# Later keys and counts, and thirteen transfers issued by other engines, in a sparse attention layer on one core

## The chip, the core and the metric

The kernel runs on one core of one Trainium2 chip. TensorE (PE) multiplies matrices, VectorE (DVE), ScalarE (ACT) and GpSimd (POOL) work on tiles in SBUF, and SyncE (SP) issues transfers. ScalarE and GpSimd can issue transfers too; the rows ACTq, POOLq and SPq of a profile are the instruction queues of these engines. Each engine takes its instructions in order and waits for others by semaphores, so a waiting instruction holds up all that stands behind it on its engine. The metric is the device time of one execution in microseconds (us), lower is better.

## The reference

The layer normalizes x (2708 rows of 1024, float32), clips it at zero, and lets each row attend to its neighbours in a sparse 0/1 matrix `adj` of 2708 x 2708, whose entries are one with probability 0.0014771, so about four to a row:

```python
h = jnp.maximum(_layernorm(x, axis=-1), 0.0)
q = h @ W_q.T + b_q;  k = h @ W_k.T + b_k;  v = h @ W_v.T + b_v
z = scale * (q @ k.T) * adj
z = jnp.where(z == 0.0, -10000.0, z)
out = x + relu(softmax(z, axis=1) @ v)
```

(The last lines are shortened to the same computation.)

## The kernel before, in words

Rows come in 22 tiles of 128 (the last has 20). The kernel never forms k or v. It first multiplies the two weights into one 1024 x 1024 matrix M (rows of `wq` and `wk` are loaded in eight pieces each, `wq_sb[o]` and `wk_sb[o]`), so that a row's q is h M plus a row made from the biases. The two bias columns `bk_sb` and `bq_sb` are loaded by GpSimd at the start; VectorE scales them (L508, L509) and sums the pieces of `wk` with them into `acc_b`. Beside that it runs small set-up operations (L155 to L182).

At the same time the neighbours are found. Tiles of `adj` are loaded in the order SEARCH. For the tile at place k of it, `counted(k)` lets ScalarE sum the ones, `found(k)` lets VectorE find up to eight ones in each quarter of a row (L376), and `listed(k)`, at the end of a batch of up to four tiles, merges them into a row's sorted list of keys (L389 to L395). `counts` then counts each row's neighbours and prepares a table row: up to 16 neighbours, the row's number, the count (L645 to L653). `sort` finds each row's position by its count, with two small matmuls on TensorE (L662, L664); `put` (L613) scatters the table rows to `tab_dram` in this order, and `reload` (L625) brings the sorted table back, for the early eight tiles and the other fourteen apart. From there, a tile holds rows with about as many neighbours.

The products are done for pairs of tiles, in ten units n of kind q (q = h M) and ten of kind o (the output weight), one tile alone at the end. `multiply` does each pair in a seven-product scheme on 2 x 2 blocks: `blocks` forms sums of the input blocks (`s1` to `s4`, L688) from transposed tiles, of which ScalarE copies some (`a11`, `a12`, `a22`, L684) and one stays in PSUM; the products' results are joined on VectorE (for q at L1029 and L1032). Units 0 to 3 take tiles 0 to 7 in their natural order, later ones gather sorted rows of h.

Attention runs as a stream beside the products (`attention`, moved on by `advance`): for a sorted tile it gathers each row's neighbours into slots g (L597), takes their products with q (`scores`, L826), an exponential on ScalarE, and the weighted sum u (`weights`, `sums`, L871 and L879). A finished u is kept in SBUF if its output unit is near, else it is stored to `u_dram` by GpSimd (L888) and loaded again by SyncE (`or`, L1142). Ten are stored. Gathers from `h_dram` and the scatter of the results to `out` are GpSimd's.

What stands where is partly written out by hand: `steps_at[n, i]` is a string of steps that `follow` carries out after the i-th point of unit n. A letter is a step and the number its place: `f` found and listed, `i` found alone, `j` listed alone, `p` counted, `c` counts, `o` sort, `w` put, `z` and `b` reload, `g` a sum of squares. The order on VectorE is the order of the program there; that of SyncE and of PE comes from a scheduler that goes by its own estimates, and GpSimd's is partly held.

Of the kernel before, what the change touches and what calls it, by code (L numbers as in the profile page):

```python
# [18 lines left out]
P = 128  # L19
# [10 lines left out]
EARLY = 8  # L30
# [33 lines left out]
def tile_preln_masked_attention(  # L64
# [366 lines left out]
            ts_done[:] = [nc.vector.tensor_sub(t[k], a, b)]  # L431

    with tc.tile_pool(name="w", bufs=1, side="left") as wp:
        nc.gpsimd.dma_start(bk_sb, bk)
        nc.gpsimd.dma_start(bq_sb, bq)
        wq_sb = [wlow[:, o] for o in range(H)] + [wp.tile([P, D], FT, name=f"wq{o}") for o in range(H, DC)]
        wk_sb = [wlow[:, H + o] for o in range(H)] + [wp.tile([P, D], FT, name=f"wk{o}") for o in range(H, DC)]
        for o in range(DC):
            nc.sync.dma_start(wq_sb[o], wq_rows[o * P:(o + 1) * P, :])
            part = slice(0, NB) if o == 0 else slice(0, D)  # L440
            (nc.scalar if o < 2 else nc.sync).dma_start(wk_sb[o][:, part], wk_rows[o * P:(o + 1) * P, part])
            if o == 1:
                nc.scalar.dma_start(wk_sb[0][:, NB:], wk_rows[:P, NB:])

        t1 = [work.tile([P, D], FT, tag="hT", name=f"t1_{k}", bufs=2) for k in range(2)]

# [174 lines left out]
    def reload(lo, hi):  # L621

        full = min(hi, FULL)
        src = tab_dram[lo >= EARLY]
        loads = [nc.gpsimd.dma_start(ptab[:, lo:full, :], src[:(full - lo) * P, :].rearrange("(t p) w -> p t w", p=P))]  # L625
        if hi > FULL:
            loads.append(nc.gpsimd.dma_start(ptab[:REST, FULL, :], src[(FULL - lo) * P:, :]))
        for load in loads:
            for put in puts[lo >= EARLY]:
                tc.add_manual_dep(load.ins, put.ins.name,  # L630
                                  mybir.DependencyInfo(mybir.DependencyClass.Sync, mybir.DependencyReason.DATA),
                                  reason="every row of the part")
        return loads[-1]
# [82 lines left out]
    def natural_rows(n):  # L716
# [23 lines left out]
    steps_ahead = {(1, 5): "o1", (3, 6): "o0"}  # L740

    slots, free = [], []
# [1 line left out]
    def searched():  # L744
        search.close()

        att = ph.enter_context(tc.tile_pool(name="att", bufs=1, side="right", reuse_waits="tile"))
        for i in range(HIGH):
            slots.append(att.tile([P, D], FT, name=f"g{i}"))


        for c in range(4):
            for k, (i, j) in enumerate(((0, 0), (0, 1), (1, 1), (1, 0))):
                nc.sync.dma_start(slots[2 * c + k // 2][:, k % 2 * NB:(k % 2 + 1) * NB], wv[j][:, i * 4 + c, :])
        assert len(adj_loads) == NT
        free.extend([M.rearrange("p i j (a c) w -> p i j a (c w)", a=2)[:, 0, 1, a, :] for a in range(2)] + slots[8:])
# [118 lines left out]
    def sums(t):  # L875
        u, coef = us.pop(t)
        for s in range(0 if t in EMPTY else 1, K[t]):
            fill()
            chained(lambda: nc.vector.scalar_tensor_tensor(  # L879
                u, g_of[t][s], coef[:, at[t][s]:at[t][s] + 1], u, op0=ALU.mult, op1=ALU.add))  # L880
            free.append(g_of[t][s])
            yield 1.3
        fill()
        g_of.pop(t)
        if near(t):
            held[t] = u
        else:
            nc.gpsimd.dma_start(u_dram[t * P:(t + 1) * P, :], u)  # L888
        done.add(t)

    def marked(lo, hi):
# [268 lines left out]
    for n, unit in enumerate(units):  # L1160
        kind, ta, tb = unit
        now[0] = n
        if n == FIRST:
            ordered.close()
            ordered.enter_context(tc.manual_schedule(engines={mybir.EngineType.DVE}))
            nc.sync.dma_start(bp_dram, bp_sb[0:1, :])
        turn = n in (0, FIRST - 1)
        share = (20.0 if kind == "q" else 19.0) / 7
        nxt = units[n + 1] if n + 1 < len(units) else None
        results = (q_results if kind == "q" else o_results)(ta, tb)  # L1170

        def after(i):
            if (n, i) in steps_ahead:
                follow(steps_ahead[n, i])
            if (n, i) == (2, 5):
                owe(8)
                owe(9)
                rows_of[FIRST] = load_rows(units[FIRST])
                owe(10)
                owe(6)  # L1180
                owe(7)
                rows_of[FIRST + 1] = load_rows(units[FIRST + 1])
                pooled.close()
            if (n, i) in ((FIRST, 1), (FIRST, 5)):
                ts_of_wv(i // 2, i // 2 + 2)
            if (n, i) == (FIRST, 5):
                next(stream)
            if (n, i) == (FIRST, 6):
                chain.append(behind[-1])
                next(stream)  # L1190
                nc.vector.tensor_tensor(bad, bad, total, op=ALU.not_equal)
            if (n, i) == (FIRST + 1, 6):
                marked(EARLY, NT)
            if (n, i) == (FIRST + 2, 4):
                nc.vector.tensor_scalar(msq, msq, MLIMIT, None, op0=ALU.is_gt)
            if n > FIRST + 1 or n == FIRST + 1 and i > 1:
                advance(share)
            if nxt is not None:

                if i == (3 if n == 0 else 4 if turn else 0):  # L1200
                    ops_of[n + 1] = blocks(*rows_of[n + 1], nc.gpsimd if n + 1 < FIRST - 1 else None)
                    with tc.issue_after(products[-1].ins) if n + 1 == FIRST else nullcontext():
                        ops_of[n + 1][1]()
                if i == (4 if n == 0 else 5 if turn else 2):
                    ops_of[n + 1][2]()
                    rows_of.pop(n + 1)
                    if n == last_q - 1:
                        all_rows()
                if i == 3:
                    banks_of[n + 1] = banks_for(bp_sb)  # L1210
                if i == 6 and n + 2 < FIRST:
                    natural_rows(n + 2)
                if i == (2 if n in (FIRST, last_q) else 4) and n + 2 > FIRST and n + 2 < len(units) and n + 2 not in rows_of:
                    while units[n + 2][0] == "o" and not done.issuperset(units[n + 2][1:]):
                        advance(1.0)
                    rows_of[n + 2] = load_rows(units[n + 2])
            if (n, i) in steps_at:
                follow(steps_at[n, i])
            if (n, i) == (3, 4):
                searched()  # L1220
                for s in range(8, HIGH):
                    for c in range(0, D, D // 4):
                        clear = nc.gpsimd.memset(slots[s][:, c:c + D // 4], 0.0)
                        tc.add_manual_dep(clear.ins, counted_at[-1].ins.name,
                                          mybir.DependencyInfo(mybir.DependencyClass.Sync, mybir.DependencyReason.DATA),
                                          reason="not beside the counts")
            if i == 3 and units[n - 1][0] == "o" and NT - 2 in units[n - 1][1:]:
                tail(NT - 1)
            if nxt is None and i == 1:
                while alone not in done:  # L1230
                    advance(1.0)
                r, = load_rows(("o", alone))
                single["turned"] = turned(r, "alone")
            if nxt is None and i == 3:
                single["banks"] = banks_for(bp_sb)
            if n == last_q - 1 and i == 4:

                nc.sync.dma_start(bp_sb, bv.to_broadcast([P, D]))
                nc.vector.tensor_sub(bp_sb[:, NB:], bp_sb[:, NB:], bp_sb[:, :NB])

            for k, at in enumerate(((0, 0), (0, 1), (0, 3), (0, 4), (0, 5), (0, 6), (1, 2))):
                if (n - last_q, i) == at:
                    place, src = ((M[:, 0, 0], of_wv(0, 0)), (T[:, 0], tv_dram[0]), (T[:, 1], tv_dram[1]),
                                  (M[:, 1, 0], of_wv(1, 0)), (M[:, 1, 1], of_wv(1, 1)), (T[:, 2], tv_dram[2]),
                                  (T[:, 3], tv_dram[3]))[k]
                    nc.sync.dma_start(place, src)

        multiply(n, results, after)
# [231 lines left out]
```

## Time and profile before

| | |
|---|---|
| time, median of three runs | 648.64 us (646.54 to 648.71) |
| profiled execution, its time | 648.43 us |
| its span | 646.7 us |
| TensorE busy | 636.7 us, 98% |
| VectorE busy | 523.1 us, 81% |
| GpSimd busy | 400.1 us, 62% |
| ScalarE busy | 280.0 us, 43% |
| transfers | 189.02 MB, mean 292 GB/s |
| granted clock of TensorE, mean | 0.996 |
| chain of waits, share of the span | PE 75%, DVE 15%, DMA 6% |

The span runs from the first to the last instruction of the profiled execution; the time also holds what lies around it. A row of the timeline gives start, length, engine, line and operation, what it writes and reads, and in brackets how long its engine was idle ahead of it and what ended that. DMA issues are listed with the number of transfers, the size of each and the time from issue to landing. The engine of a matmul's weights is PEld.

### The profile page before, as it was taken

The numbers are of one execution on the slowest core, as the hardware profiler recorded it, in microseconds if no ns is written. First come the engines' busy times: TensorE is split into PE (matmuls) and PEld (weight loads), VectorE is DVE, ScalarE is ACT, GpSimd is POOL, SyncE is SP. The second block draws the span as 40 slices with busy tenths as digits, with TensorE's granted clock in tenths as the row PEclk, the third lists the DMA queues.
The fourth block names the chain that finished last, engine by engine and source line by source line (L and its number), as shares of the span: only waits on it lengthen the run. The fifth ranks groups of instructions, "written<-read, shape, count | busy, mean of one in ns | idle before, by whom it ended". The sixth has DMA issues, their size and how long they took to land.

```text
span 646.7 us, 6378 instructions
## 1 busy us (share of the span) xinstructions
PE 636.7 (98%) x1730; PEld 326.6 (51%) x1730; DVE 523.1 (81%) x1014; ACT 280.0 (43%) x426; POOL 400.1 (62%) x428
## 2 busy tenths in 40 slices
PE   9999999999999899999999999999999999999995
PEld 5777776454444445444444454444544544444442
DVE  5999599997896664999888969987999999988121
ACT  3448876858766532323223133332432434323200
POOL 2649990885767457865845536655785858782431
PEclk9999999999999999999999999999999999999998
DMA  8994999599799969998877999988898989884641
GB/s 337 407 355 143 391 342 393 202 322 353 244 343 311 360 196 402 352 374 263 302 277 267 419 414 315 289 264 261 242 332 274 289 297 322 256 281 122 168 140 69
DMA packets 61012, 189.02 MB, mean 292 GB/s; under 512 B 9711, under 2 KB 10047, under 8 KB 60074
## 3 DMA queue, kind: packets, MB, share of 16 engines
q0 software_dynamic: 31728, 98.74, 46.4%
q1 hardware_dynamic: 27514, 84.04, 35.1%
q10 hardware_dynamic: 1728, 5.77, 2.3%
q8 instruction: 16, 0.26, 0.2%
q14 instruction: 26, 0.21, 0.1%
HBM read 159.81 MB, written 42.31 MB: 313 GB/s over the span
## 4 chain that ended last, share of the span: by engine, by line
PE 75%; DVE 15%; DMA 6%; issue 2%; POOL 1%; ACT 0%; POOLq 0%; SPq 0%; DVEq 0%
PE ps L948 41%; PE psy L948 29%; DMA adj<-in_adj_dram 5%; PE pt L402 5%; DVE at L376 5%; DVE acc_b L519 2%; DVE st L224 1%; DMA bq_sb<-in_bq_dram 1%; DVE wlow L530 1%; DVE wlow L431 1%; DVE M L481 1%; DVE wlow L528 1%; DVE cand L394 1%; DMA h_dram<-x 0%; DVE s L688 0%
## 5 line engine op out<-in xcount | busy, mean ns | idle before, releaser
L597 POOL DMA_INDIRECT g<-h_dram,tab x105 | 127.0, 1209 | 60.7 <-issue 21.6
L948 PE MATMUL ps<-M,a 128*128 128x512 f32 x320 | 144.0, 593 | 0.1
L948 PE MATMUL psy<-wlow,s 128*128 128x512 f32 x320 | 143.9, 593 | 0.0
L826 DVE SCALAR_TENSOR_TENSOR junk<-g,pq 128x1024 uint8<-128x1024 f32 x93 | 113.7, 1223 | 7.6 <-DMA g<-h_dram,tab 5.7
L879 DVE SCALAR_TENSOR_TENSOR u<-g,coef,u 128x1024 f32<-128x1024 f32 x79 | 101.3, 1283 | 5.6 <-ACT u L871 3.6
L948 PEld LDWEIGHTS ps<-M,a 128*128 128x128 f32 x320 | 59.4, 190 | 68.2 <-issue 67.6
L948 PEld LDWEIGHTS psy<-wlow,s 128*128 128x128 f32 x320 | 59.3, 190 | 67.2 <-issue 66.8
L376 DVE FIND_INDEX8 at<-ones,adj 128x8 uint32<-128x685 f32 (+1 forms) x88 | 74.5, 865 | 0.0
L948 PE MATMUL ps<-wlow,s 128*128 128x512 f32 x160 | 72.0, 593 | 1.7 <-DVE s L688 1.7
L948 PE MATMUL psy<-wlow,a 128*128 128x512 f32 x160 | 72.2, 593 | 0.0
L948 PE MATMUL ps<-M,s 128*128 128x512 f32 x160 | 71.9, 592 | 0.0
L355 ACT ACTIVATE sized<-adj 128x2708 uint8<-128x2708 f32 (+1 forms) x22 | 54.3, 2467 | 13.7 <-DMA adj<-in_adj_dram 12.8
L1047 POOL DMA_INDIRECT y<-in_x_dram,tab x19 | 35.0, 1840 | 28.7 <-ACT y L1064 12.1
L285 POOL TENSOR_TENSOR hsum<-hsum,x 128x256 f32<-128x256 f32 (+1 forms) x56 | 38.6, 727 | 21.6 <-DVE wlow L431 15.6
L948 PEld LDWEIGHTS ps<-wlow,s 128*128 128x128 f32 x160 | 30.3, 190 | 40.3 <-issue 37.3
L948 PEld LDWEIGHTS psy<-wlow,a 128*128 128x128 f32 x160 | 30.4, 190 | 37.8 <-issue 37.3
L948 PEld LDWEIGHTS ps<-M,s 128*128 128x128 f32 x160 | 30.4, 190 | 37.8 <-issue 37.3
L778 POOL DMA_INDIRECT out_dram<-y,tab x21 | 29.8, 1419 | 18.1 <-DMA y<-in_x_dram,tab 10.5
L597 POOL DMA_INDIRECT M<-h_dram,tab x20 | 25.6, 1281 | 13.3 <-ACT u L871 4.6
L684 ACT COPY a<-pt 128x512 f32<-128x512 f32 x60 | 33.3, 589 | 1.1 <-PE pt L402 1.1
L613 POOL DMA_INDIRECT tab_dram<-tab,pos_i x22 | 22.4, 1017 | 17.5 <-DVE pos_i L673 12.0
L688 DVE TENSOR_TENSOR s<-a,pt 128x512 f32<-128x512 f32 x40 | 25.6, 680 | 6.7 <-ACT a L684 6.7
(240 smaller groups left out, 863.8 us busy)
## 6 DMA issues: line engine op xcount, KB each, us to landing
adj<-in_adj_dram SPq DMA_DIRECT2D x21, 1354.0 KB, 10.8
x<-in_x_dram SPq DMA_DIRECT2D x21, 512.0 KB, 7.4
h_dram<-x POOLq DMA_DIRECT2D x16, 512.0 KB, 7.4
q_late<-q SPq DMA_DIRECT2D x12, 512.0 KB, 6.4
pq<-q_late SPq DMA_DIRECT2D x12, 512.0 KB, 6.3
u_dram<-u POOLq DMA_DIRECT2D x10, 512.0 KB, 7.2
or<-u_dram SPq DMA_DIRECT2D x10, 512.0 KB, 7.6
g<-in_wv_dram SPq DMA_DIRECT2D x16, 256.0 KB, 9.6
```

Source lines behind the costliest of these rows:

```text
L285: small.append(nc.gpsimd.tensor_add(hsum[:n, cols], hsum[:n, cols], xt[:n, cols]))
L355: nc.scalar.activation(sized[:n], a[:n, :, :PW], AF.Abs, accum_out=total[:n, t:t + 1])
L376: nc.vector.max_index(at[:n, k - first_k, g, :], ones[:n, 0:8], a[:n, g, :])
L402: nc.tensor.transpose(pt[:, c, :], xt[:, k * P:(k + 1) * P], ident)
L597: return nc.gpsimd.indirect_dma_start(out=dst, out_offset=None, in_=src, in_offset=off, bounds_check=N - 1, oob_is_err=False)
L684: nc.scalar.copy(ops[name], bank)
L688: step = (eng or nc.vector).tensor_tensor(ops[name], a, b, op=op)
L778: to = nc.gpsimd.indirect_dma_start(out=out, out_offset=bass.IndirectOffsetOnAxis(ap=ptab.bitcast(U32)[:n, t, SLOTS:SLOTS + 1], axis=0), i ...
L826: chained(lambda: nc.vector.scalar_tensor_tensor(junk, g_of[t][s], 1.0, tq[t], op0=ALU.mult, op1=ALU.mult, accum_out=zall[:, t, s:s + 1]))
L879: chained(lambda: nc.vector.scalar_tensor_tensor(u, g_of[t][s], coef[:, at[t][s]:at[t][s] + 1], u, op0=ALU.mult, op1=ALU.add))
L948: mm = nc.tensor.matmul(bank, a[:, c, :], b[:, c, :], start=False, stop=(c == 3), skip_group_check=True)
L1047: return nc.gpsimd.indirect_dma_start(out=y[:n], out_offset=None, in_=x, in_offset=off, compute_op=ALU.add)
```

## The change

Four things are changed:

- The listing of the last batch of keys and the counts of the early half move in unit 3. The search of the last `adj` tile stays at (3, 1), its listing goes to (3, 5), and the counts go there from (3, 2). The zeroing of three gather slots, which waits for the counts, goes from (3, 4) to (3, 5).
- The two biases are loaded by ScalarE, behind its three loads of `wk`, instead of by GpSimd.
- The early table is loaded by SyncE instead of by GpSimd; the other table stays with GpSimd.
- The stores of u are issued by SyncE instead of by GpSimd.

```diff
     with tc.tile_pool(name="w", bufs=1, side="left") as wp:
-        nc.gpsimd.dma_start(bk_sb, bk)
-        nc.gpsimd.dma_start(bq_sb, bq)
...
             if o == 1:
                 nc.scalar.dma_start(wk_sb[0][:, NB:], wk_rows[:P, NB:])
+                nc.scalar.dma_start(bk_sb, bk)
+                nc.scalar.dma_start(bq_sb, bq)
...
-        loads = [nc.gpsimd.dma_start(ptab[:, lo:full, :], src[:(full - lo) * P, :].rearrange("(t p) w -> p t w", p=P))]
+        loads = [(nc.gpsimd if lo >= EARLY else nc.sync).dma_start(ptab[:, lo:full, :], src[:(full - lo) * P, :].rearrange("(t p) w -> p t w", p=P))]
...
-                (3, 1): "f21", (3, 2): "c0", (3, 3): "p21", (3, 5): "g0", (3, 6): "w0-7 g1 g2 g3 g4", (4, 4): "b0"}
+                (3, 1): "i21", (3, 3): "p21", (3, 5): "j21 c0 g0", (3, 6): "w0-7 g1 g2 g3 g4", (4, 4): "b0"}
...
         else:
-            nc.gpsimd.dma_start(u_dram[t * P:(t + 1) * P, :], u)
+            nc.sync.dma_start(u_dram[t * P:(t + 1) * P, :], u)
...
             if (n, i) == (3, 4):
                 searched()
+            if (n, i) == (3, 5):
                 for s in range(8, HIGH):
                     for c in range(0, D, D // 4):
                         clear = nc.gpsimd.memset(slots[s][:, c:c + D // 4], 0.0)
```

On VectorE, in unit 3, behind the search of the last `adj` tile, two pieces of the difference (the number behind a tile's name is a buffer's; `cand` are the candidates of a row, `q` the results of tiles 6 and 7, `s` the sums for the next pair):

```order
 L376 MAX_INDEX at<-ones,adj_155 128x8 x4
+L1032 TENSOR_TENSOR q_1351<-ps_1257,u_1362 128x512
+L1029 TENSOR_TENSOR q_1352<-psy,p_1335 128x512
+L688 TENSOR_TENSOR s_1442<-a_1435,pt 128x512
+L688 TENSOR_TENSOR s_1444<-a_1385,pt 128x512
+L688 TENSOR_TENSOR s_1446<-s_1442,a_1385 128x512
+L688 TENSOR_TENSOR s_1448<-a_1392,s_1446 128x512
 L389 TENSOR_TENSOR cand<-first,at 128x128
 L390 SCALAR_TENSOR_TENSOR cand<-at,cand 128x128
```

The two results and the four sums now stand right behind the search. Where they stood, behind the last operation of the counts and ahead of the sort, is this piece:

```order
 L650 TENSOR_TENSOR sort<-deg,down 128x144
 L653 TENSOR_SCALAR tab<-keys 128x8x16
-L1032 TENSOR_TENSOR q_1351<-ps_1257,u_1377 128x512
-L1029 TENSOR_TENSOR q_1352<-psy,p_1335 128x512
-L688 TENSOR_TENSOR s_1477<-a_1470,pt 128x512
-L688 TENSOR_TENSOR s_1479<-a_1408,pt 128x512
-L688 TENSOR_TENSOR s_1481<-s_1477,a_1408 128x512
-L688 TENSOR_TENSOR s_1483<-a_1415,s_1481 128x512
 L666 COPY sort<-ps_all 128x144
```

The twenty-one rows of keys and counts, from L389 to L653, have changed places with six rows of results and sums.

On VectorE at the start, the set-up operations among the sums with the biases (`t` are differences of halves of `wk`):

```order
 L525 TENSOR_TENSOR t_0_199<-wlow 128x512
 L519 SCALAR_TENSOR_TENSOR acc_b<-wlow,bq_sb,acc_b 128x1024
+L155 CAST tab<-zall 128x22
+L158 CAST past<-zall 128x22
+L165 CAST down<-zall 128x20
+L181 CAST first<-zall 128x32
+L159 TENSOR_SCALAR past<-past 128x22
 L525 TENSOR_TENSOR t_0_199<-wlow 128x512
+L182 MEMSET zall 128x352
```

These six stood ahead of the first operation that reads a bias, and now stand behind the second sum with them.

On SyncE, near the end, where three of the ten stores of u now stand (u_3325, u_3438 and u_3493 are those of tiles 20, 18 and 19; `or` are loads of stored u, of the same tiles in the same order; `pq` are loads of q for the scores):

```order
 L799 DMA pq_3351<-q_late 128x1024
 L799 DMA pq_3406<-q_late 128x1024
+L888 DMA u_dram<-u_3325 128x1024
 L799 DMA pq_3445<-q_late 128x1024
+L888 DMA u_dram<-u_3438 128x1024
 L1142 DMA or_3557<-u_dram 128x1024
+L888 DMA u_dram<-u_3493 128x1024
 L1142 DMA or_3700<-u_dram 128x1024
 L1142 DMA or_3702<-u_dram 128x1024
```

The store of tile 18 now stands ahead of the load of tile 20, and that of tile 19 ahead of the load of tile 18.

## The prediction

> **What bounds the kernel now.** I read the page first, then the busy time by stretch, then what TensorE waited for, then the rows around that wait. The page says how full each engine is:
>
> ```profile
> span 646.7 us, 6378 instructions
> PE 636.7 (98%) x1730; PEld 326.6 (51%) x1730; DVE 523.1 (81%) x1014; ACT 280.0 (43%) x426; POOL 400.1 (62%) x428
> ```
>
> A busy PE is not yet a PE at its pace, so I take the stretches (us, then busy time of PE, PEld, DVE, ACT, POOL, then the granted clock, DMA share, GB/s) and the waits of PE (total, times, longest):
>
> ```profile
> 106.00:212.00 106.00, 104.27 (x296) 49.58 (x295) 92.31 (x256) 75.00 (x94) 75.37 (x119) 1.00 0.86 305
> 212.00:630.00 418.00, 418.00 (x1162) 198.98 (x1163) 338.67 (x549) 137.88 (x247) 253.28 (x205) 1.00 0.85 288
> ...
> PE ps L948 <- DVE s L688: 1.7, 1, 1.7
> PE ps_y L498 <- POOL hsum L112: 1.2, 1, 1.2
> ```
>
> From 212 to 630 us TensorE is busy for 418.00 of 418.00 us at a clock of 1.00: there, nothing that VectorE, GpSimd or a transfer does earlier can shorten the kernel. Before that PE waits twice: 1.2 us at the very start, for a memset, and 1.7 us once, for VectorE's s. The change can win at this second wait, and else it can only lose. These are the rows of that place on PE and on VectorE (start, length, what; the idle time ahead in brackets):
>
> ```profile
> 206.59 3.60 PE L948 MATMUL ps<-M,a 128*128 128x512 f32 x8
> 211.86 3.70 PE L948 MATMUL ps<-wlow,s 128*128 128x512 f32 x8 [1.67 <-DVE s L688]
> 215.40 3.60 PE L948 MATMUL psy<-wlow,a 128*128 128x512 f32 x8
> 218.84 0.23 PE L662 MATMUL ps_in<-sort,before 128*128 128x144 bf16 x1
> ...
> 205.29 0.29 DVE L389 TENSOR_TENSOR cand<-first,at 128x128 f32<-128x128 f32 x1
> ...
> 209.80 0.22 DVE L653 TENSOR_SCALAR tab<-keys 128x128 uint32<-128x128 f32 x1
> 209.94 0.68 DVE L1032 TENSOR_TENSOR q<-ps,u 128x512 f32<-128x512 f32 x1
> 210.54 0.68 DVE L1029 TENSOR_TENSOR q<-psy,p 128x512 f32<-128x512 f32 x1
> 211.13 1.27 DVE L688 TENSOR_TENSOR s<-a,pt 128x512 f32<-128x512 f32 x2
> ```
>
> The last keys and the early counts (L389 to L653) hold VectorE from 205.29 to 209.94, 4.65 us, and q and s, for which PE waits, stand behind them.
>
> **Part 1: keys and counts behind the sums.** Undisturbed, a group of eight on PE follows the one before it after 3.44 us (215.40 to 218.84). After the group at 206.59 the next could start at 210.03; it starts at 211.86, 1.83 late. The following group starts 3.54 after it, 0.10 more than the pace. So this place costs 1.93 us. With q and s moved to 205.29, what bounds s is ScalarE's copy and the transposes ahead of it:
>
> ```profile
> 206.35 0.58 ACT L684 COPY a<-pt 128x512 f32<-128x512 f32 x1 [1.05 <-PE pt L402]
> ```
>
> It ends at 206.93, and by then the two q (2 x 0.6 us from 205.29) are through. The first s ends about 0.68 later, at 207.6, 2.4 us ahead of 210.03: the wait goes whole. What is late next? The keys and counts then run from about 209.7 (four operations on s at 0.65, half of the 1.27 that two take, from 206.9) to 214.3. The sort's matmul, which needs the counts, stands on PE behind two groups, at 210.03 + 2 x 3.44 = 216.9. That leaves 2.6 us. GpSimd's zeroing of three gather slots, which waits for the counts, and its writing of the table rows stand here:
>
> ```profile
> 210.13 3.09 POOL L1223 MEMSET g<- 128x256 f32 x12 [2.36 <-ACT junk_m L362]
> 221.93 1.21 POOL L613 DMA_INDIRECT tab_dram<-tab,pos_i  x1 [8.71 <-DVE pos_i L673]
> ```
>
> The zeroing moves to 214.3 to 217.4, and the row positions come 1.9 us earlier with PE, at about 219.6, so it hides in GpSimd's own 8.71 us of idle time. Term: **-1.93 us**.
>
> **Part 2: the biases from ScalarE's queue.** VectorE waits for them at the start (rows of the timeline, and between them the issues of weights: KB each, us to landing):
>
> ```profile
> 1.73 0.45 ACTq L443 DMA_DIRECT2D wlow<-in_wk_dram  x1
> ...
> 3.04 0.19 DVE L155 CAST tab<-zall 128x22 uint32<-128x22 int32 x1 [0.85 <-POOL zall L153]
> 3.73 0.35 DVE L182 MEMSET zall<- 128x352 f32 x1
> 5.51 1.06 ACT L492 ACTIVATE junk_w<-wlow 128x1024 uint8<-128x1024 f32 x1 [2.02 <-DMA wlow<-in_wq_dram]
> 5.31 0.33 SPq L441 DMA_DIRECT2D wlow<-in_wk_dram  x1
> 5.63 14.77 PE L463 MATMUL ps_x<-wlow 128*128 128x512 f32 x32
> 9.92 0.17 DVE L508 TENSOR_SCALAR bq_sb<-bq_sb 128x8 f32<-128x8 f32 x1 [5.84 <-DMA bq_sb<-in_bq_dram]
> ...
> wq<-in_wq_dram SPq DMA_DIRECT2D x4, 512.0 KB, 9.6
> wlow<-in_wk_dram ACTq DMA_DIRECT2D x2, 256.0 KB, 4.5
> ...
> 107.94 1.27 DVE L688 TENSOR_TENSOR s<-a,pt 128x512 f32<-128x512 f32 x2
> 110.69 3.60 PE L948 MATMUL ps<-wlow,s 128*128 128x512 f32 x8
> ```
>
> No row has a small load behind ScalarE's three weight loads. ScalarE had issued those by 2.18; two more at up to 0.45 each end by 3.1, and that fits into the 2.02 us for which it idles before 5.51 anyway: nothing. The landing lies between 3.1 + 4.5 = 7.6 us (the ACT-queue row) and 3.1 + 9.6 = 12.7 (the SP-queue row), against 9.9 now. I take about 10, near now's, since they queue behind 1 MB of weights. The order also puts six set-up operations, 3.04 to 4.08 = 1.0 us, from that wait to behind it. So VectorE runs between 1.3 us earlier and 3.8 us later than before, and I take 1 later. PE does not feel an earlier VectorE, and a later one only where it first needs s: that is ready at 108.6 and used at 110.69, 2.1 us of cover. Term: 0, at most +1.7.
>
> SyncE keeps few loads in flight: its sixth waited until 5.31 for a landing. With the two biases among those in flight, already its fourth, the third piece of wk, waits until then. At worst it lands 9.6 later, at 14.9, and PE, which reads it from the middle of its 32 records on (5.63 + 7.4 = 13.0), waits 1.9. I take 0, because the data of SyncE's three loads ahead of it have to pass first in either kernel.
>
> The Trainium skill speaks against this part: in "DMA: Bandwidth & Descriptors", section "Queues, rings and completion order", descriptors of one issuing queue are served in ring order on each DMA engine. By that the biases land behind all of ScalarE's weights, and the sum stays what it is.
>
> **Part 3: the early table's load from SyncE.** GpSimd's row, and the loads of the late and the early table among the issues:
>
> ```profile
> 235.13 0.95 POOL L625 DMA_DIRECT2D tab<-tab_dram  x1 [2.50 <-DMA tab_dram<-tab,pos_i]
> ...
> tab<-tab_dram POOLq DMA_DIRECT2D x1, 117.0 KB, 6.3
> tab<-tab_dram POOLq DMA_DIRECT2D x1, 72.0 KB, 3.1
> ```
>
> On SyncE it waits for the same eight table writes, and holds up a store of q_late and four slots' tv_dram stores, which nothing reads before the output products. It may come up to 2.9 us earlier (1.93 with the positions, 0.95 of GpSimd's issue) or some 3 later if its 72-byte pieces land slowly (6.3 us, as the late table's load, instead of 3.1). Either way it only moves the attention stream, inside the stretch where PE is full: 0.
>
> **Part 4: ten stores of u from SyncE.** The group of these stores on GpSimd (busy, mean ns, idle before), and the loads that read them back:
>
> ```profile
> L888 POOL DMA_DIRECT2D u_dram<-u x10 | 5.8, 583 | 1.8 <-DMA g<-h_dram,tab 1.0 <-DVE u L879 0.7
> ...
> or<-u_dram SPq DMA_DIRECT2D x10, 512.0 KB, 7.6
> ```
>
> GpSimd gets 5.8 us back, all of it in the stretch where PE waits for nothing: 0. SyncE, which issues in order, now waits for each u before it may issue what stands behind. For nine of the ten the u is ready before SyncE issued that next entry anyway. The tightest of the nine, and the tenth:
>
> ```profile
> 305.77 1.28 DVE L879 SCALAR_TENSOR_TENSOR u<-g,coef,u 128x1024 f32<-128x1024 f32 x1
> 309.32 0.32 SPq L1022 DMA_DIRECT2D q_late<-q  x1
> ...
> 540.53 0.32 SPq L1142 DMA_DIRECT2D or<-u_dram  x1
> 540.53 2.61 DVE L879 SCALAR_TENSOR_TENSOR u<-g,coef,u 128x1024 f32<-128x1024 f32 x2
> 555.88 1.04 PE L402 MATMUL pt<-ident,or 128*128 128x128 f32 x8
> ```
>
> In the tightest u is done at 307.05 and the next entry came at 309.32. The tenth is u of tile 18 (L879 at 540.53, done 543.1), and behind it stands the load of tile 20's row block, issued at 540.53 until now. At 543.1 + 7.6 = 550.7 it has landed. PE transposes it at 555.88 - 1.93 = 553.95: 3.2 us of cover. Term: 0.
>
> **Sum.** The profiled execution took 648.43 us, 1.7 around its span of 646.7. 648.43 - 1.93 = **646.5**. The median of the three runs, 648.64, is 0.2 above the profiled one, and they spread from 646.54 to 648.71; by the median the forecast would be 646.7.
>
> **Rivals.** *SyncE blocked, slower.* An entry of SyncE's queue is held up by a u ahead of it until PE waits; nearest to that is the load of tile 20 behind the store of tile 18's u. It decides once that load lands more than 10.8 us after 543.1. This is what the transfers of that tensor took:
>
> ```profile
> DMA to landing us min/median/max: 3.5/7.4/16.0
> ```
>
> For: if the load is served only once the store ahead of it has landed, it lands at 543.1 + 7.4 + 7.6 = 558.1, and PE waits 4.2: 650.7; with a store as long as the longest, 12.8: 659.3. I take the middle, 8.5: **655.0**, slower than before. Against: transfers of one queue overlap everywhere in this trace (SyncE's loads at the start are issued before the earlier ones land), and VectorE may be earlier.
>
> By the skill's ring rule (same section) the load would lie straight behind that store's 512 KB on one ring, where until now the store went by GpSimd's: an estimated 1.8 us more at the 288 GB/s of that stretch, cover 1.4 instead of 3.2, sum unchanged.
>
> *A late start.* VectorE is 3.8 us later and PE waits 1.7 at its first s: 648.2; with the third piece of wk at its worst, 1.9: 648.4.
>
> *The wait stays.* Something else than VectorE's order keeps s back; the copy at 206.35 speaks against it. 648.4, as before.
>
> *More than the wait.* Nothing on PE but these two waits is worth over a microsecond, so only the spread of runs reaches here: the lowest of the three, 646.54, less 1.93 is 644.6.
>
> **Numbers.** Forecast 0.67, SyncE blocked 0.16, late start 0.06, wait stays 0.06, more 0.05. The likeliest's own range is 644.6 to 647.7; taking in the late start, the unchanged time and the mild end of the SyncE case gives 644.6 to 649.8. About 0.5%, 3.2 us, is what a measurement of this kernel tells from no change. The forecast lies inside it; faster by more needs the low end of the runs (0.10: the last rival, and 0.05 of the forecast for its own spread), slower by more needs a stall of over 5.2 us (0.11: the upper two thirds of the SyncE case, which begins at 4.2), and 0.79 is left for same.
>
> **What would show it.** Right: PE has no wait on s L688 near 210 us, its sort matmul comes near 216.9, the stretch to 630 stays full, and the span is about 644.8. Wrong: a PE row with idle time at an s near 110 (biases), at a transpose of `or` near 554 (SyncE), or at the sort's matmul near 217 (counts too late).

## The result, and the profile after

The changed kernel took 648.38 us (median of 22 runs, 646.72 to 654.57), the kernel before 648.12 (22 runs, 645.87 to 652.30). The ratio is 1.0006 with a 95% interval of 0.9990 to 1.0022: no change. The profiled execution after took 647.12 us with a span of 645.4, 1.3 less than before. The measured time lies inside the range of the forecast, but the forecast itself, 1.9 us faster, lies outside the interval (0.6 us faster to 1.4 slower): its one term, -1.93 us, is not in the medians, and the 1.3 us of the profile come from a place that the prediction never looked at. Where the expected gain went is what the experiments are about.

Page, stretches and waits of TensorE of the changed kernel, beside the one stretch of before that the prediction did not show (first row of the second fence):

```profile
span 645.4 us, 6398 instructions
PE 636.8 (99%) x1730; PEld 326.0 (51%) x1730; DVE 522.3 (81%) x1014; ACT 279.2 (43%) x426; POOL 380.2 (59%) x415
...
10.00:106.00 96.00, 94.37 (x220) 67.72 (x219) 84.79 (x171) 61.76 (x78) 62.35 (x84) 1.00 0.85 322
106.00:212.00 106.00, 105.94 (x310) 51.19 (x309) 93.51 (x246) 76.01 (x95) 73.57 (x111) 1.00 0.87 316
212.00:630.00 418.00, 418.00 (x1163) 198.72 (x1162) 340.77 (x570) 137.88 (x248) 238.76 (x201) 1.00 0.86 289
...
PE ps_v L581 <- DVE M L481: 1.6, 2, 1.2
PE ps_y L498 <- POOL hsum L112: 1.2, 1, 1.2
```
```profile
10.00:106.00 96.00, 96.00 (x237) 69.88 (x236) 87.81 (x176) 63.55 (x82) 64.58 (x84) 1.00 0.88 338
```

The wait for s is gone from the list, and another stands in its place: TensorE was full from 10 to 106 us and now loses 1.6 there. These are the places. First the one that the change was read for (TensorE, VectorE, then GpSimd, after):

```profile
208.50 3.60 PE L948 MATMUL ps<-M,a 128*128 128x512 f32 x8
211.94 3.60 PE L948 MATMUL ps<-wlow,s 128*128 128x512 f32 x8
218.81 0.23 PE L662 MATMUL ps_in<-sort,before 128*128 128x144 bf16 x1
...
208.88 1.28 DVE L688 TENSOR_TENSOR s<-a,pt 128x512 f32<-128x512 f32 x2 [0.36 <-ACT a L684]
215.69 0.31 DVE L650 TENSOR_TENSOR sort<-deg,down 128x144 bf16<-128x144 f32 x1
...
221.90 1.20 POOL L613 DMA_INDIRECT tab_dram<-tab,pos_i  x1 [2.57 <-DVE pos_i L673]
```

The group on s follows its predecessor after 3.44 us, the pace. But it starts at 211.94, where before it started at 211.86: TensorE comes 1.91 us later to this place, and the removed wait only makes up for that. Here is where it fell behind. VectorE's start and the issues of ScalarE and SyncE (after, then VectorE's first moments L224 before and after):

```profile
2.21 0.76 ACTq L442 DMA_DIRECT2D bk_sb<-in_bk_dram  x1
3.00 0.52 ACTq L443 DMA_DIRECT2D bq_sb<-in_bq_dram  x1
5.33 0.33 SPq L439 DMA_DIRECT2D wlow<-in_wk_dram  x1
12.54 0.17 DVE L508 TENSOR_SCALAR bq_sb<-bq_sb 128x8 f32<-128x8 f32 x1 [10.38 <-DMA bq_sb<-in_bq_dram]
...
38.66 1.27 DVE L224 BATCH_NORM_STATS2 st<-x 128x6 f32<-128x512 f32 x2
42.22 1.28 DVE L224 BATCH_NORM_STATS2 st<-x 128x6 f32<-128x512 f32 x2
```

The biases land at 12.5 us instead of 9.9, and at L224 VectorE is 3.56 us late: 2.62 from the landing and 0.94 from what comes behind it, about 0.8 of that the six set-up operations that now stand there. It does not catch up. TensorE feels it first at 36 us, where it loads operands that VectorE's L528 has made (the engine's weight loads, after; L528 ends at 36.06, before at 31.72):

```profile
36.11 0.97 PEld L463 LDWEIGHTS ps_z<-t,wlow 128*128 128x128 f32 x3 [0.47 <-DVE wlow L528]
```

That adds only 0.16 us to TensorE's lateness. The large loss is at 92 us. The products that make M pass through PSUM banks that VectorE (L481) and ScalarE (L477) empty; the sums of the bias row, ps_v (L581), go into banks that L481 has to empty first. Before, then after:

```profile
90.37 2.05 DVE L481 SCALAR_TENSOR_TENSOR M<-ps_z,M 128x256 f32<-128x256 f32 x6
92.33 1.88 PE L581 MATMUL ps_v<-acc_b,ones 128*128 128x512 f32 x4
...
94.14 2.05 DVE L481 SCALAR_TENSOR_TENSOR M<-ps_z,M 128x256 f32<-128x256 f32 x6
93.52 1.10 PE L581 MATMUL ps_v<-acc_b,ones 128*128 128x512 f32 x2 [1.22 <-DVE M L481]
95.02 1.10 PE L581 MATMUL ps_v<-acc_b,ones 128*128 128x512 f32 x2 [0.40 <-DVE M L481]
```

Before, the first two of the six end near 91.1, and the second ps_v started at 92.33 + 0.86 = 93.2: 2.1 us of cover (the time from when something is ready to when it is used). VectorE is 3.77 later here, so 1.7 us have to show, 1.9 with TensorE 0.2 earlier at this place; its lateness grows by 2.11.

The 1.3 us of the span lie behind the last matmul. GpSimd's last transfer and its DRAIN at the end of the program (shortest, median and longest of three, ns), before and after:

```profile
640.62 0.96 POOL L1280 DMA_INDIRECT out_dram<-y_alone,half_i  x1 [1.67 <-DVE y_alone L1296]
L1476 POOLq DRAIN  x3: 46/115/4727, 641.1 to 646.5; - x3
...
640.69 0.97 POOL L1281 DMA_INDIRECT out_dram<-y_alone,half_i  x1 [1.67 <-DVE y_alone L1297]
L1477 POOLq DRAIN  x3: 46/118/3346, 641.2 to 645.1; - x3
```

The last result leaves 0.07 us later than before, and the program ends 1.3 us earlier, since the DRAIN takes 3.35 us instead of 4.73.

### The profile page after: what moved, and what is told of

It is laid out like the page before. It is cut to its first block, busy times and chain, and to the rows that moved or that the text cites. A ratio compares the mean times of both kernels' runs of the same rounds, so it can differ in the third digit from the quotient of the medians.

```text
span 645.4 us, 6398 instructions
## 1 busy us (share of the span) xinstructions
PE 636.8 (99%) x1730; PEld 326.0 (51%) x1730; DVE 522.3 (81%) x1014; ACT 279.2 (43%) x426; POOL 380.2 (59%) x415
## 4 chain that ended last, share of the span: by engine, by line
PE 84%; DMA 7%; DVE 7%; POOL 1%; issue 0%; ACT 0%; ACTq 0%; SPq 0%; POOLq 0%; DVEq 0%
PE ps L948 45%; PE psy L948 32%; PE pt L402 5%; DVE at L376 2%; DMA x<-in_x_dram 2%; DMA adj<-in_adj_dram 2%; PE ps_y L463 2%; DMA bq_sb<-in_bq_dram 1%; DVE st L224 1%; DMA wk<-in_wk_dram 1%; DVE acc_b L519 1%; DVE M L481 1%; DMA h_dram<-x 1%; PE ps_h L1153 0%; DVE wlow L528 0%
## 5 line engine op out<-in xcount | busy, mean ns | idle before, releaser
L597 POOL DMA_INDIRECT g<-h_dram,tab x105 | 124.0, 1181 | 69.0 <-issue 21.3
L1047 POOL DMA_INDIRECT y<-in_x_dram,tab x19 | 33.0, 1738 | 33.1 <-ACT taken L1013 12.8
L778 POOL DMA_INDIRECT out_dram<-y,tab x21 | 26.7, 1274 | 18.4 <-DMA y<-in_x_dram,tab 10.8
L597 POOL DMA_INDIRECT M<-h_dram,tab x20 | 24.0, 1201 | 14.6 <-ACT u L871 4.7
L263 ACT ACTIVATE x<-x,r 128x1024 f32<-128x1024 f32 (+1 forms) x22 | 25.9, 1235 | 9.9 <-POOL r L253 9.9
```

Of the source, the lines that this page charges most:

```text
L263: nc.scalar.activation(xs[i][:n], xs[i][:n], AF.Relu, bias=r[:n, 4, i:i + 1], scale=r[:n, 3, i:i + 1])
L597: return nc.gpsimd.indirect_dma_start(out=dst, out_offset=None, in_=src, in_offset=off, bounds_check=N - 1, oob_is_err=False)
L778: to = nc.gpsimd.indirect_dma_start(out=out, out_offset=bass.IndirectOffsetOnAxis(ap=ptab.bitcast(U32)[:n, t, SLOTS:SLOTS + 1], axis=0), i ...
L1047: return nc.gpsimd.indirect_dma_start(out=y[:n], out_offset=None, in_=x, in_offset=off, compute_op=ALU.add)
```

## The experiments

TensorE does the same 1730 matmuls in the same order in every kernel here, so the lateness of each against the profile of before can be read off directly. It changes at few places only. The table gives it behind each (us; minus is earlier), and the tail from the last matmul's end to the span's end. In before's own profile 1.94 us are lost at s, so a kernel that loses nothing there gains 1.94 in that column. The start is no work of the changes: in before's profile the first two matmuls on the weights took 1.22 and 0.88 us instead of 0.59, and its second profile is 0.82 earlier there. The step at 36 us has no column; it is 0.16 to 0.23 us in the four profiles with the biases behind ScalarE's weights and 0.9 in late_vector.

| kernel | start, 7 us | ps_v, 94 | transposes, 107 | sort, 151 | s, 212 | last matmul | tail |
|---|---|---|---|---|---|---|---|
| before | 0 | 0 | 0 | 0 | 0 | 0 | 7.12 |
| after | -0.36 | +1.91 | +1.91 | +1.91 | -0.03 | +0.08 | 5.73 |
| keys_only | -0.65 | -0.65 | -0.65 | -0.65 | -2.54 | -2.25 | 7.12 |
| biases_only | -0.81 | +0.23 | +4.44 | +4.44 | +4.44 | +4.45 | 6.95 |
| biases_back | -0.83 | -0.83 | +1.12 | +1.50 | -0.44 | -0.44 | 5.81 |
| biases_first | +1.75 | +1.75 | +1.75 | +1.75 | +0.02 | +0.02 | 5.74 |
| late_vector | -0.30 | +2.48 | +2.48 | +3.40 | +1.69 | +1.78 | 5.82 |
| roots_ahead | -0.58 | -0.58 | -0.58 | +0.27 | -1.66 | -1.55 | 5.82 |
| roots_ahead_2 | -0.72 | -0.72 | -0.72 | -0.72 | -2.66 | -2.66 | 5.82 |
| before_again | -0.82 | -0.82 | +1.30 | +1.70 | +0.56 | +0.78 | 7.12 |
| after_again | -0.80 | +0.85 | +2.60 | +2.60 | +0.65 | +0.65 | 5.73 |
| roots_none | -0.71 | -0.71 | -0.71 | -0.71 | -2.36 | -2.36 | 7.12 |
| roots_keys | -0.45 | +0.34 | +0.34 | +2.04 | +0.11 | +0.11 | 7.12 |
| roots_all | -0.85 | +2.32 | +2.32 | +2.73 | +0.98 | +0.98 | 5.75 |

The times (medians; the ratio is to the runs of before made with it):

| kernel | us (lowest to highest) | ratio, 95% interval |
|---|---|---|
| keys_only | 646.24 (645.64 to 648.59) | 0.9962, 0.9942 to 0.9982 |
| biases_only | 652.72 (649.76 to 656.02) | 1.0063, 1.0037 to 1.0088 |
| biases_back | 646.65 (644.89 to 649.82) | 0.9975, 0.9955 to 0.9995 |
| biases_first | 649.06 (646.80 to 650.72) | 1.0009, 0.9989 to 1.0029 |
| late_vector | 648.86 (647.68 to 652.92) | 1.0019, 1.0001 to 1.0037 |
| roots_ahead | 644.85 (644.46 to 645.59) | 0.9958, 0.9942 to 0.9974 |
| roots_ahead_2 | 644.87 (644.40 to 646.51) | 0.9968, 0.9957 to 0.9979 |
| roots_none | 647.42 (646.08 to 648.82) | 0.9989, 0.9972 to 1.0006 |
| roots_keys | 646.16 (645.68 to 648.54) | 0.9979, 0.9967 to 0.9992 |
| roots_all | 647.78 (645.14 to 650.46) | 0.9999, 0.9984 to 1.0014 |

**keys_only**: before with part 1.

```diff
-                (3, 1): "f21", (3, 2): "c0", (3, 3): "p21", (3, 5): "g0", ...
+                (3, 1): "i21", (3, 3): "p21", (3, 5): "j21 c0 g0", ...
...
+            if (n, i) == (3, 5):
```


> Part 1 alone: the last keys and the early counts behind the third pair's sums, everything else as before. Theory A (two waits of TensorE in a row, of which the second was the size of the first): the wait of 1.94 us at s near 210 us goes and nothing takes its place, because the biases still land near 9.9 us and VectorE is as early at 92 us as before. Lost time of TensorE 3.26 - 1.94 = 1.3 us, last matmul near 637.7 us, about 1.9 us (0.3%) faster than before. Theory B (the gain at 210 us never reaches the end, whatever happens earlier): lost time goes down, but the last matmul stays near 639.6 us and the time is the same as before.

Measured: 1.9 us under before by the medians (interval of the ratio 1.2 to 3.8 us), and the profile loses nothing at ps_v or at s. Theory A holds, B falls: beside these runs of before, part 1 is worth what the prediction said, if nothing else changes.

**biases_only**: before with part 2.

```diff
-        nc.gpsimd.dma_start(bk_sb, bk)
-        nc.gpsimd.dma_start(bq_sb, bq)
...
                 nc.scalar.dma_start(wk_sb[0][:, NB:], wk_rows[:P, NB:])
+                nc.scalar.dma_start(bk_sb, bk)
+                nc.scalar.dma_start(bq_sb, bq)
```


> Part 2 alone: the biases from ScalarE's queue, everything else as before. Theory A (VectorE has caught up by 205 us and holds s there until a fixed time, so that a wait ahead of it is swallowed by the wait at s): biases land near 12.5 us, TensorE waits about 2.1 us for a PSUM bank at 92 to 95 us, and the wait at s near 210 us shrinks from 1.94 to about 0.1. Lost time stays 3.2 to 3.4 us, same time as before. Theory C (the waits add up): lost time 3.26 + 2.1 = 5.3 us, 2 us (0.3%) slower than before.

Measured: 4.5 us slower, more than either theory. The wait for the PSUM bank at ps_v is there (0.85 us), the wait at s has not shrunk, and a third one, at the transposes, takes 4.2:

```profile
107.22 0.66 PE L402 MATMUL pt<-ident,x 128*128 128x128 f32 x4 [2.48 <-ACT M L477]
108.67 1.52 PE L402 MATMUL pt<-ident,x 128*128 128x128 f32 x11 [0.80 <-ACT M L477]
...
216.31 1.98 PE L948 MATMUL ps<-wlow,s 128*128 128x512 f32 x4 [1.69 <-DVE s L688]
```

That the biases cost is shown; that VectorE always holds s until the same time is not. The third wait had to be explained.

**biases_back**: the changed kernel with the two loads on GpSimd as before (the diff above, reversed).

> The changed kernel with the biases back on GpSimd's queue (parts 1, 3 and 4). Theory A: lost time of TensorE 1.3 us, last matmul near 637.7 us, 1.9 us faster than before and than the changed kernel, the same as part 1 alone. Theory B: same as before. If the load and the stores on SyncE cost something that the changed kernel's own wait hid, it shows here as a wait of TensorE between 230 and 560 us that part 1 alone does not have.

Measured: 1.5 us under before (interval 0.3 to 2.9 us), not the 3.2 that part 1 and the tail together make. The bank wait is gone; the third wait is here too, without any bias on ScalarE. ScalarE empties its bank late because GpSimd delivers late the scales with which ScalarE normalizes its rows (nine small operations, L246 to L254; ScalarE waits for the eighth, L253). Rows of GpSimd, VectorE, ScalarE and TensorE in biases_back, then in before:

```profile
93.76 2.28 POOL L251 TENSOR_TENSOR r<-r 128x2 f32<-128x2 f32 x1
98.59 1.08 POOL L254 TENSOR_SCALAR msq<-r 128x2 f32<-128x2 f32 x1
93.64 2.35 DVE L431 TENSOR_TENSOR wlow<-M 128x1024 f32<-128x1024 f32 x2
98.54 2.37 ACT L263 ACTIVATE x<-x,r 128x1024 f32<-128x1024 f32 x2 [8.77 <-POOL r L253]
105.35 1.63 PE L402 MATMUL pt<-ident,x 128*128 128x128 f32 x12 [0.80 <-ACT M L477]
74.12 0.35 DVE L389 TENSOR_TENSOR cand<-first,at 128x128 f32<-128x128 f32 x1
...
93.72 0.20 POOL L251 TENSOR_TENSOR r<-r 128x2 f32<-128x2 f32 x1
94.60 0.22 POOL L254 TENSOR_SCALAR msq<-r 128x2 f32<-128x2 f32 x1
94.88 2.33 DVE L431 TENSOR_TENSOR wlow<-M 128x1024 f32<-128x1024 f32 x2
94.55 2.37 ACT L263 ACTIVATE x<-x,r 128x1024 f32<-128x1024 f32 x2 [4.59 <-POOL r L253]
74.30 1.42 DVE L389 TENSOR_TENSOR cand<-first,at 128x128 f32<-128x128 f32 x1
74.27 1.29 POOL L560 TENSOR_TENSOR wk<-wk,wlow 128x512 f32<-128x512 f32 x1
```

In before the ninth operation ends at 94.82 and VectorE's first L431 starts at 94.88, 0.06 us behind it. In biases_back L431 comes 1.24 earlier, and L251, 0.20 us long, takes 2.28: it waits for two L431 to end, and L252 to L254 wait for one each. ScalarE gets its scales 4 us later. And 1.1 of VectorE's 1.24 us come from 74 us: there its L389 slipped in ahead of a GpSimd operation (L560) at 74.12, while in before it came 0.03 us behind it and waited 1.1. The third wait goes with this race: of the nine profiles of kernels with the nine operations in their old place, those four in which L389 took 0.29 to 0.35 us here (biases_only, biases_back, before_again, after_again) have the wait at the transposes, and those five in which it took 0.99 to 1.42 (before, after, keys_only, biases_first, late_vector) do not. So the 4.2 us of biases_only are not the price of the biases alone. The Trainium skill, "SBUF — State Buffer", section "SBUF: two separate sides", calls the port pair that VectorE and GpSimd share an exclusive lock, held for a whole instruction by whichever starts first (of VectorE's operations, those with two SBUF inputs are among the ones that take it); these rows agree.

The DRAIN's 1.3 us do not show between the medians of keys_only and biases_back, 646.24 and 646.65. The times of each fall into groups 1 to 3 us apart (nine of 645.6 to 646.3 and three of 648.1 to 648.6; three of 644.9 to 645.7, eight of 646.3 to 647.1 and one of 649.8). That fits a race that most runs of the one win and most of the other lose, but only one run of each was profiled, so it is not shown.

**biases_first**: the two loads ahead of ScalarE's three weight loads.

```diff
+        nc.scalar.dma_start(bk_sb, bk)
+        nc.scalar.dma_start(bq_sb, bq)
         wq_sb = ...
...
                 nc.scalar.dma_start(wk_sb[0][:, NB:], wk_rows[:P, NB:])
-                nc.scalar.dma_start(bk_sb, bk)
-                nc.scalar.dma_start(bq_sb, bq)
```


> The changed kernel with the two bias loads issued by ScalarE ahead of its three weight loads instead of behind them. If a queue's loads are served in the order of issue, the biases land well before 9.9 us (4 to 7), VectorE starts its weights 2 to 4 us earlier than in the kernel before, the first weights land up to 1 us later, and TensorE starts that much later: lost time 1.3 to 2.3 us, 0.9 to 1.9 us faster than before. If it is the small loads themselves that are slow, wherever they stand, they land at 9 us or later and the wait at 92 to 95 us stays near 2 us.

```profile
5.50 0.17 DVE L508 TENSOR_SCALAR bq_sb<-bq_sb 128x8 f32<-128x8 f32 x1 [3.34 <-DMA bq_sb<-in_bq_dram]
12.13 0.75 DVE L517 TENSOR_SCALAR acc_b<-wlow,bq_sb 128x1024 f32<-128x1024 f32 x1 [5.53 <-DMA wlow<-in_wk_dram]
8.05 1.22 PE L463 MATMUL ps_x<-wlow 128*128 128x512 f32 x2 [2.41 <-DMA wlow<-in_wk_dram]
```

The same loads land at 5.5 instead of 12.5, so it is their place in the queue that decides. But TensorE starts on the weights 2.4 us later, where I expected at most 1. ScalarE issues its first weights 0.9 us later (1.73 instead of 0.83); the rest is behind the two loads of 4 KB in the queue. VectorE does not start its weights earlier either: L517 waits for a piece of `wk` until 12.13 (10.95 before). The kernel is no faster than before.

**late_vector**: biases_back with VectorE made late.

```diff
                 if o == 0:
-                    nc.vector.tensor_scalar(acc_b, wk_sb[o], bq_sb[:, 0:1], None, op0=ALU.mult)
+                    for _ in range(6): nc.vector.tensor_scalar(acc_b, wk_sb[o], bq_sb[:, 0:1], None, op0=ALU.mult)
```


> Parts 1, 3 and 4 with the biases on GpSimd's queue as before (the kernel biases_back), and VectorE made late on purpose: the first product of the bias row (L517) is computed six times over instead of once, 5 x 0.67 to 0.75 = 3.4 to 3.8 us, about the lateness that the changed kernel shows at its first moments (42.22 against 38.66). Theory A (VectorE's lateness alone makes the wait that ate the gain): TensorE loses 2 us or more between 92 and 108 us, at the PSUM banks of ps_v (L581) or at the transposes behind them (L402), and the time is that of the changed kernel, 648.4, or above it. Theory D (the loss came from the weight pieces that SyncE issued 3 us later, not from VectorE): less than 0.5 us is lost there beside what biases_back loses, and the time is biases_back's, 646.7.

```profile
10.81 4.70 DVE L517 TENSOR_SCALAR acc_b<-wlow,bq_sb 128x1024 f32<-128x1024 f32 x6
94.09 1.10 PE L581 MATMUL ps_v<-acc_b,ones 128*128 128x512 f32 x2 [1.00 <-DVE M L481]
95.59 1.10 PE L581 MATMUL ps_v<-acc_b,ones 128*128 128x512 f32 x2 [0.41 <-DVE M L481]
```

Six in 4.70 us instead of one in 0.76: 3.9 us later, and 1.9 us appear at the same ps_v as in the changed kernel (and 0.9 at 36 us, again behind L528), 2.2 us above biases_back in the median, 2.9 by the ratios to before. Theory A holds; the weight pieces that SyncE issues later are not needed for it.

**before_again, after_again**: each kernel once more, for a second profile.

> The kernel before once more, for a second profile of it. Theory E: where this run is faster or slower than the first profile's 648.43 by over 1 us, the difference stands at TensorE's transposes and banks between 92 and 108 us, and goes with the time at which GpSimd's row scales end; elsewhere TensorE's starts agree within 0.3 us. Theory F: it is spread over the run or lies at its end.

> The changed kernel once more, for a second profile of it. Theory A: the biases land near 12.5 us again, VectorE is 3 to 4 us behind the kernel before at 42 us, and TensorE loses 2 us or more between 92 and 108 us, at ps_v, at the transposes or at both; near 212 us it does not wait. Theory D or chance: the biases land at another time, or nothing is lost there.

In before_again (649.21 us, 0.8 above the first profile, less than the 1 us that the expectation asked for) the race fell the other way: L389 starts at 74.36, 0.06 us ahead of L560, L254 ends at 99.84, and TensorE loses 2.1 us at the transposes. Further 1.2 us go at the sort, near 186 and near 203 us, more than theory E allowed outside 92 to 108. Being late, TensorE does not wait at s at all, though part 1 is not in this kernel. In after_again (647.70 us) the biases land at 12.27, and 1.4 us are lost at ps_v and 1.75 at the transposes.

**roots_ahead**, run twice: biases_back with the nine operations ahead of the last sum of rows on GpSimd.

```diff
         normed[first] = group, xs, r
+        if first == 2: nc.gpsimd.tensor_add(hsum, hsum, last_sum.pop())
...
             if add:
-                nc.gpsimd.tensor_add(hsum[:n], hsum[:n], xt[:n])
+                last_sum.append(xt) if t == 18 else nc.gpsimd.tensor_add(hsum[:n], hsum[:n], xt[:n])
...
-    owed = {}
+    owed, last_sum = {}, []
```


> The kernel biases_back with one more move: on GpSimd the nine small operations on the row scales (L246 to L254, near 92 us) come ahead of the last of the four sums of rows (L272, 2.37 us) instead of behind it. Theory E (the runs differ because these small operations end within 0.1 us of VectorE's first L431, and whoever is late there waits for the other engine's long operations): the scales end 2.4 us earlier, always ahead of L431; ScalarE scales its rows by 95 us at the latest, TensorE does not wait at the transposes near 104 us, lost time 1.1 to 1.4 us, last matmul near 637.2, median 645.0 to 646.0, and a narrower spread than biases_back's 644.9 to 649.8. Theory F (the wait at the transposes has another cause): median and spread as biases_back's, 646.7.

> Roots_ahead once more (parts 1, 3 and 4, biases as before, row scales ahead of the last sum of rows), since it took 644.85 where the same without parts 3 and 4 took 646.16 beside another chip's runs of before. In roots_keys's profile TensorE lost its 0.8 and 1.7 us at ps_v near 93 and at the sort near 151 us, ahead of every instruction that parts 3 and 4 touch. If that difference is chance of the run or the chip, this takes 644.5 to 646.5, and its profile shows waits at ps_v, at the sort or at neither, as they fall; if parts 3 and 4 help, it stays within 0.3 of 644.85.

```profile
92.43 0.22 POOL L254 TENSOR_SCALAR msq<-r 128x2 f32<-128x2 f32 x1
92.60 2.39 POOL L256 TENSOR_TENSOR hsum<-hsum,x 128x1024 f32<-128x1024 f32 x1
92.38 2.37 ACT L263 ACTIVATE x<-x,r 128x1024 f32<-128x1024 f32 x2 [2.51 <-POOL r L253]
103.63 1.91 PE L402 MATMUL pt<-ident,x 128*128 128x128 f32 x16
```

No wait at the transposes (the rows are of roots_ahead_2, whose TensorE loses nothing against before behind its start). The medians are 644.85 and 644.87, on two chips, with spreads of 1.1 and 2.1 us against 4.9 for biases_back. This is the best kernel found, 0.3 to 0.4% under before, and it has parts 1, 3 and 4 but not 2.

**roots_none, roots_keys, roots_all**: the same move with none of the change, with part 1, and with all of it.

> The kernel before with the row scales ahead of the last sum of rows (as in roots_ahead) and none of the change's parts. Roots_ahead, which has parts 1, 3 and 4, took 644.85. Theory E with part 1 worth its 1.93: TensorE waits at s near 210 us as in the kernel before and nowhere between 92 and 108 us; median 644.85 + 1.93 = 646.8, spread under 1.5 us. If part 1 was only worth what the spread of runs makes it seem: 645 to 646.

> The same with part 1 alone. If the load of the table and the stores on SyncE cost and bring nothing (parts 3 and 4), the time is that of roots_ahead, 644.85, within 0.3. If they cost something that the spread hid, it is below 644.5; if they bring something, above 645.2.

> The same with all four parts, the biases on ScalarE's queue among them. Theory A: the biases land near 12.4 us, VectorE is 3.1 to 3.6 us late at 42 us, TensorE loses 1.5 to 2.1 us at ps_v near 92 us and does not wait at the transposes near 104 us; median 644.85 + 1.5 to 2.1 = 646.4 to 647.0, so that part 1 and part 2 cancel. If the price of the biases was only the race near 95 us, it is gone here: 644.9.

By the medians part 1 is worth 647.42 - 646.16 = 1.3 us, parts 3 and 4 646.16 - 644.86 = 1.3, and the biases cost 647.78 - 644.86 = 2.9. By the ratios to before it is 0.6, 1.0 and 2.3. Roots_ahead ran on other chips, and the intervals of roots_none and roots_keys overlap, so these sizes are rough, and part 1's is here hardly clear of nothing. The sum, +0.4 or +0.6, agrees with the changed kernel's own +0.3 against before (interval -0.6 to +1.4).

Roots_none came out above its forecast (647.42 against 646.8, a spread of 2.7 us against 1.5), and roots_all too (647.78 against 646.4 to 647.0; its profile loses 3.0 us at ps_v, not 1.5 to 2.1). Why part 1 is under 1.93 here, roots_none's profile suggests: L389 of the last keys starts at 202.93, 2.4 us earlier than before, and s is hardly waited for. Of the four profiles of kernels without part 1, the wait at s is whole in two (before, biases_only) and nearly or wholly gone in two (roots_none 0.3 us, before_again 0).

```profile
202.93 0.29 DVE L389 TENSOR_TENSOR cand<-first,at 128x128 f32<-128x128 f32 x1
209.51 3.70 PE L948 MATMUL ps<-wlow,s 128*128 128x512 f32 x8
```

These kernels still spread over 2.7 to 5.3 us, though none waits at the transposes. In roots_keys's profile, its slowest run, VectorE waits 2.3 us for a block of `adj` near 90 us, and TensorE loses 0.8 at ps_v and 1.7 at the sort. So the meeting of GpSimd and VectorE that theory E named is one source of the spread, not the only one.

## Why the prediction was right, and where it was not

"No change" was right, but not for its reasons. A gain of 1.93 us was forecast that is too small to stand out from the spread; measured is no gain. Part 1 won its gain or somewhat less, part 2 cost more than that, and the end of the program gave 1.3 back. That these nearly cancel is luck. None of the three signs of being wrong that the prediction named (idle time at an s near 110, at a transpose of `or` near 554, at the sort's matmul near 217) showed: the loss stood at a fourth place.

*Part 1, -1.93.* The mechanism is as written: the first s is ready at 209.57, 2.4 us ahead of its use, as forecast, though at another time (207.6 was forecast; q waits for TensorE first). The counts' sums end at 216.0, 2.8 us ahead of the sort's matmul (2.6 forecast; the matmul comes at 218.8, not 216.9, because TensorE is late), and the zeroing hides. The size holds for an execution like the profiled one. The median gain was 1.9 beside before and 1.3 beside roots_none (0.6 by the ratios). In two of four profiles without part 1 there is hardly a wait to remove, since TensorE is later or VectorE earlier at 210 us; that this makes the medians differ fits, and is not shown for the other runs. A wait seen in one profile was taken as one of every run.

*Part 2, 0, at most +1.7.* This step failed, twice. The landing was taken as 10 from inside bounds of 7.6 and 12.7, "near now's"; it was 12.5. The rule of the Trainium skill that the prediction quoted ("DMA: Bandwidth & Descriptors", section "Queues, rings and completion order": one queue's loads in ring order) said behind all of ScalarE's weights. Biases_first and the changed kernel agree with it, 5.5 and 12.5 (and in the changed kernel SyncE's issues that wait for ScalarE's loads start in that order, at 5.3, 7.9 and 9.9 behind the three weights and at 11.2 and 12.5 behind the biases); yet it was let stand with the sum unchanged. And the cover was looked for at the wrong place: "PE does not feel an earlier VectorE, and a later one only where it first needs s" overlooked two earlier hand-overs: the operands from L528 at 36 us, which cost 0.16, and the PSUM banks, which TensorE needs from VectorE at 92 us, which cost 2.11. By the medians of roots_all and roots_ahead part 2 costs 2.9 us in all, by their ratios 2.3, where +1.7 was the most that was allowed for. The first half of the quoted sentence fails too: in biases_back an earlier VectorE cost TensorE 1.95 us. The "late start" rival, with a chance of 0.06, had the right cause and lateness (3.8 us; 3.56 measured), but put the wait at the first s, where TensorE does not wait. That its time, 648.2 to 648.4, meets the median is luck: it has no 1.3 us from the end of the program in it.

SyncE's fourth load did wait until 5.33, as forecast, and 0 was right for it: TensorE's lateness does not change between its start and 36 us, where it waits for VectorE. ScalarE's two issues took 0.76 and 0.52 us instead of up to 0.45 each, and still fit into its idle time.

*Parts 3 and 4, 0.* Right on TensorE, and the most likely rival fell. The store of tile 18's u and the load behind it, and the transposes that need it:

```profile
543.74 0.32 SPq L888 DMA_DIRECT2D u_dram<-u  x1
544.15 0.43 SPq L1142 DMA_DIRECT2D or<-u_dram  x1
...
555.96 1.04 PE L402 MATMUL pt<-ident,or 128*128 128x128 f32 x8
```

The load is issued 3.6 us later than before, and TensorE does not wait. Wrong at the end: GpSimd's DRAIN is shorter by 1.3 us in every kernel with these parts, and no cover hides that. "GpSimd gets 5.8 us back, all of it in the stretch where PE waits for nothing: 0" stopped at the stretch where TensorE is full.

*Sum* of the profile: -0.36 (start, not of the change) + 0.16 (36 us) + 2.11 (ps_v) - 1.94 (s) + 0.11 (behind s, not looked into) = +0.08 at the last matmul, and -1.39 behind it: -1.31, which is the measured change of the span.

## What to carry to other kernels

When an edit makes an engine later, search every hand-over from it for the first that has too little cover, from its first operands for TensorE on, the emptying of PSUM banks included. Before a removed wait is booked as gain, see whether it is there in a second profile of the same kernel: lateness elsewhere can swallow it. And price a moved DMA at both ends of the program: behind what it queues at the start, and what its issuer still has to clear up at the end.

## What the runs showed of the hardware

GpSimd's DRAIN at the end grows with the plain (not indirect) DMAs that GpSimd issued in the program: 32 gave 4.72 to 4.73 us, 30 gave 4.56, 21 gave 3.41 to 3.43, 19 gave 3.34 to 3.35, in all 14 profiles, so 0.04 to 0.13 us for each one saved. In before the last store of u had landed at 556.74, 84 us ahead of it. What the engine does in that time stays open, and so does whether the number of DMAs counts or their kind: the table's load and the ten stores were never moved apart.

Two loads of 4 KB, 8 numbers for each of 128 partitions, at the head of ScalarE's queue made TensorE start 2.4 us later on the weights behind them, 0.9 of it in the issue.

An earlier engine made the kernel slower: VectorE 1.2 us earlier shut out GpSimd's small operations for 4 us and cost TensorE 1.95 us. The same kernel fell either way from run to run: L389 and L560 start 0.03 us apart in before, and 0.06 us apart the other way round in before_again.
